# Biases added by TensorE from one table of three bfloat16 parts, in a graph layer with a routed feed-forward net

## The chip, the cores and the metric

The kernel runs on one core of a Trainium2 chip. The metric is the device time of one execution in microseconds (us). The engines have short names in the profile: PE (TensorE, matmuls), PEld (its weight loads), DVE (VectorE), ACT (ScalarE), POOL (GpSimd), SP (SyncE, here only a queue for transfers).

## What is computed

A graph with 3125 nodes of 256 features and 100,000 edges, sorted by destination, goes through one layer. Cut to what matters:

```python
xn = layernorm(x)
# graph part: a maximum over the edges of each node
e   = relu((xn[dst] - xn[src]) @ theta_w.T + theta_b + xn[src] @ phi_w.T + phi_b)
gnn = segment_max(e, dst)                 # 0 where a node has no edge
# mixer: attention without softmax, k and v normalised per head
mix = ((q @ (k.T @ v)) / N) @ w_out.T + b_out
x = x + gnn + mix
# feed-forward: 8 experts, the best 2 of each node, weighted
xt = layernorm(x)
logits = xt @ Wr + br
h = gelu((xt * ln_g[e] + ln_b[e]) @ W1[e] + b1[e])
y = h @ W2[e] + b2[e]
x = x + sum over the two experts of weight * y
```

Everything is float32. The biases that TensorE adds are `theta_b + phi_b`, `b_out`, `br` and the eight rows of `b2`.

## The kernel before

**Edges.** The part of an edge that depends on its source, b = xn @ (phi - theta).T, is a table in device memory (`b_d`). Each edge is a gathered row of it. A partition holds a run of consecutive edges, so a running maximum along the run, cut where the destination changes, gives each node's maximum. The edges stand in 727 columns of 128 edges, in five groups (`STEPS`), from the high nodes to the low ones. POOL gathers one column with one indirect transfer (L123) into one of five buffers of eight columns. DVE folds it into the running maximum (`fold`, L403), and SP's queue stores the full buffer to `s_d`. A buffer is free for the next gathers when its store has landed. A last set of 55 columns, of the 16 nodes with the most edges, is not gathered at all: `first_nodes` counts them by one-hot matmuls (L1119 to L1123) and `first_maxima` takes their maxima with mask matmuls in bfloat16 (L1173) and reductions on DVE (L1144).

**Nodes.** The 25 tiles of 128 nodes are taken group by group as their edges are done (`GROUPS`: tiles 18 to 24, 11 to 17, 4 to 10, 1 to 3, and 0). `mixer` (L1203 to L1231) sums k.T @ v over all tiles at the start and `mixer_product` folds it with the weights into `am_w`. `without_edges` (L439) then makes for a tile, in one PSUM bank of 512 columns, the part of the graph result that doesn't depend on edges (left half) and x plus the mixer's result (right half). It starts with the bias matmul of L444, which has one row, a weight of ones; then come four passes with `am_w` (L446) and two with the identity and x (L447). ACT copies both halves out (L450, L451). For groups 0 and 1 this runs right after the mixer's product, before the tokens; for the others after group 1's dispatch (`rest_without_edges`), before most of group 1's expert units. `token_tile` (L468) gathers the tile's last rows (`r1`), adds what was carried over between partitions (L492), normalises, and makes the router's logits, with a bias matmul of one row at L543.

**Experts.** Groups 0 to 2 are scattered by expert to device memory (L130) and come back as lots of 256 rows; group 3 is picked on chip by one-hot matmuls (L787), 128 rows for each expert; tile 0 goes densely through all eight experts. So there are 24 units of 256 rows (0 to 23), 8 of 128 (24 to 31) and 8 dense ones. A unit (`Units.run`, L685) has 8 steps; each makes 128 hidden features with matmuls into `hp` (L693) that ACT passes through gelu into `ring` (L695), and one step of the second layer of the unit before into `yp` (L717). When a `yp` is full, `done` (L875) adds the row of `b2` with a float32 matmul of 8 rows at L878: a column of the identity, spread over n columns, picks the expert. ACT copies the result to `ys` (L879), and ACT's queue stores it. The dense tile adds its biases in another way, with the shares as weights (L949).

**Order.** The order on PE, DVE, ACT and SP is the order in which the program text runs. A small planner writes it: the main loop issues a gather, moves its clock on by one tick (`TICK` is 1.25 us) and lets every task that is due issue its next instructions (`tick`, L1266). A task yields how many ticks it wants to wait. `on_pe(us)` books time on PE, and the stream of expert units (`Stream.go`, L843) yields `room()` after each step, the ticks until PE's booked time less two. So what is booked for `without_edges` (3.1 us at L448) moves the expert units in the order. Nothing is booked for the matmul of L878. POOL's gathers and scatters keep the order of issue (`behind`, L103), and so do all transfers made by `move` (L113).

**Loads.** `loads` (L1032) brings the small tensors through ACT's queue; after 20 ticks two DVE instructions (L1046, L1047) put together the bias row of `without_edges`.

Of the kernel before, what the change touches and what calls it, by code (L numbers as in the profile page):

```python
# [8 lines left out]
F32 = mybir.dt.float32  # L9
BF16 = mybir.dt.bfloat16  # L10
# [9 lines left out]
P = 128  # L20
# [4 lines left out]
D = 256  # L25
# [5 lines left out]
E = 8  # L31
# [32 lines left out]
SEATS = 3  # L64
TICK = 1.25
ROWS = 256

KEYS = 391
KR = EP // KEYS
# [2 lines left out]


@with_exitstack
def gps_layer(ctx: ExitStack, tc: tile.TileContext, x, src, dst, thetaT, phiT, gbias, wq, wkvT,
              woT, bout, wr, br, small, w12, b2, out):
    nc = tc.nc
    keep = ctx.enter_context(tc.tile_pool(name="keep", bufs=1))
    dram = ctx.enter_context(tc.tile_pool(name="dram", bufs=1, space=DRAM))
# [6 lines left out]
    def on_pe(us):  # L86
        clock["pe"] = max(clock["pe"], clock["now"]) + us / TICK
# [127 lines left out]
    to_node = keep.tile([P, G, NT], F32, name="to_node")  # L215
    through = keep.tile([P, G, P], BF16, name="through")
    am_w = keep.tile([P, 2, 2 * D], F32, name="am_w")
    bias = keep.tile([1, 2 * D], F32, name="bias")
    wr_sb = keep.tile([P, 2, E], F32, name="wr_sb")
    br_sb = keep.tile([1, E], F32, name="br_sb")  # L220
    b2_sb = keep.tile([E, D], F32, name="b2_sb")
    sm = keep.tile([P, SM, E], F32, name="sm")
    table = keep.tile([P, 1], F32, name="table")
# [210 lines left out]
    def last_rows(work, i, table):  # L434
        r1 = work.tile([P, D], F32, name="r1", bufs=4)
        gather(r1, table, end_i[:, i:i + 1])
        return r1

    def without_edges(ps, i):  # L439

        if ps is mm:
            yield from seat()
        am = ps.tile([P, 2 * D], F32, name="mm")
        nc.tensor.matmul(am, ones[0:1, :], bias, start=True, stop=False)  # L444
        for c in range(2):
            nc.tensor.matmul(am, xnT(i, c), am_w[:, c, :], start=False, stop=False)  # L446
        nc.tensor.matmul(am[:, D:2 * D], ident, x_sb[:, i, :], start=False, stop=True)  # L447
        on_pe(3.1)  # L448
        yield 3
        nc.scalar.copy(xn2(i), am[:, 0:D])  # L450
        nc.scalar.copy(x_sb[:, i, :], am[:, D:2 * D])  # L451
        if ps is mm:
            leave()
# [14 lines left out]
    def token_tile(work, ps, i, r1, slices, carried, top, top_i, newton=False, then=None,  # L468
                   also=None, at_once=None):


        xi = x_sb[:, i, :]

        def after(ticks):
            return min(ticks, at_once) if at_once else ticks

        picks = []
        for g in slices:
            picks.append(work.tile([P, P], F32, name="oh", bufs=G))
            nc.vector.tensor_scalar(picks[-1], apart, to_node[:, g, i:i + 1], None, op0=OP.is_equal)  # L480
        yield after(3)
        if also is not None:
            while "rows" not in also or "firsts" not in clock:
                yield 0.5
            nc.vector.tensor_max(r1, r1, also["rows"])
            nc.vector.tensor_max(r1[0:FIRST, :], r1[0:FIRST, :], of_first)
        yield from seat()
        r2 = ps.tile([P, D + 1], F32, name="mm")
        for k, g in enumerate(slices):
            while g not in carried:  # L490
                yield 1
            nc.tensor.matmul(r2, picks[k], carried[g], start=(k == 0), stop=(k == len(slices) - 1))  # L492
        on_pe(0.65 * len(slices))
        yield after(3)
        none = work.tile([P, 1], F32, name="none")
        nc.vector.tensor_scalar(none, r2[:, D:D + 1], -1.0, -NEG, op0=OP.add, op1=OP.mult)  # L496
        nc.vector.scalar_tensor_tensor(r1, r2[:, 0:D], none, r1, op0=OP.add, op1=OP.max)
        leave()
        nc.vector.tensor_add(r1, r1, xn2(i))
        yield 1  # L500
        nc.vector.scalar_tensor_tensor(xi, r1, 0.0, xi, op0=OP.max, op1=OP.add)  # L501
        yield 1
        mean, var = moments(work, xi, 1)

        rs = work.tile([P, 2], F32, name="rs1")
        nc.vector.tensor_scalar(rs[:, 0:1], var, EPS, None, op0=OP.add)
        nc.vector.reciprocal(rs[:, 1:2], rs[:, 0:1])
        nc.vector.tensor_scalar(rs[:, 1:2], rs[:, 1:2], var, EPS, op0=OP.mult, op1=OP.add)
        if newton:
            y = work.tile([P, 2], F32, name="root")  # L510
            for wait in roots(work, rs, y):
                if at_once != 1:
                    yield wait
            rs = y
        else:
            nc.scalar.activation(rs, rs, AF.Sqrt)
            yield after(4)
            nc.vector.reciprocal(rs, rs)
        off = work.tile([P, 1], F32, name="off")
        nc.vector.scalar_tensor_tensor(off, mean, -1.0, rs[:, 0:1], op0=OP.mult, op1=OP.mult)  # L520
        xt = work.tile([P, D], F32, name="xt")
        nc.scalar.activation(xt, xi, AF.Identity, bias=off, scale=rs[:, 0:1])
        if then:
            both = work.tile([P, 1], F32, name="both")
            nc.vector.tensor_mul(both, rs[:, 0:1], rs[:, 1:2])
            normalize(xn2(i), xi, mean, both)
            then()
        else:
            nc.scalar.activation(xn2(i), xt, AF.Copy, scale=rs[:, 1:2])
        yield after(3)  # L530
        yield from seat()
        tr = ps.tile([P, 2, P], F32, name="mm")
        for c in range(2):
            nc.tensor.transpose(tr[:, c, :], xt[:, c * P:(c + 1) * P], ident)
        on_pe(0.6)
        yield after(3)
        xtT = work.tile([P, 2, P], F32, name="xtT", bufs=1)
        nc.scalar.copy(xtT, tr)
        leave()
        yield after(2)  # L540
        yield from seat()
        lg = ps.tile([P, E], F32, name="mm")
        nc.tensor.matmul(lg, ones[0:1, :], br_sb, start=True, stop=False)  # L543
        for c in range(2):
            nc.tensor.matmul(lg, xtT[:, c, :], wr_sb[:, c, :], start=False, stop=(c == 1))
        on_pe(0.5)
        yield after(4)
        nc.vector.max(top, lg)
        nc.vector.max_index(top_i, top, lg)
        leave()  # L550
# [179 lines left out]
    class Stream:  # L730
# [112 lines left out]
        def go(self):  # L843
# [5 lines left out]
            while True:  # L849
# [21 lines left out]
                g, e = self.lots[u]  # L871
# [3 lines left out]
                def done(r, yp, u=u, ys=ys):  # L875
                    g, e = self.lots[u]
                    n = self.half(u)
                    nc.tensor.matmul(yp[0:n, :], ident[0:E, e:e + 1].to_broadcast([E, n]), b2_sb, start=False, stop=True)  # L878
                    nc.scalar.copy(ys[0:n, r, :], yp[0:n, :])  # L879
                    if r == PARTS[g] - 1:  # L880
                        at = (g * ROUND if g < G - 2 else 0) + e * CAPS[g]
                        rows = ys_d[g][at:at + CAPS[g]].rearrange("(p s) d -> p s d", p=n)
                        move(nc.scalar, rows, ys[0:n, 0:PARTS[g], :])
                        if u + 1 == len(self.lots) or self.lots[u + 1][0] != g:
                            self.through.add(g)
# [29 lines left out]
    def dense_tile(act, ps, mm, i, shared, w, next_w, order=range(E), ready=None, homes=None):  # L915
# [28 lines left out]
            nc.vector.tensor_copy(bt, bt_p)  # L944
            held["bt"] = bt

        def add_bias():
            bb = mm.tile([P, D], F32, name="mm")
            nc.tensor.matmul(bb, held["bt"], b2_sb, start=True, stop=True)  # L949
            nc.vector.tensor_add(x_sb[:, i, :], x_sb[:, i, :], bb)  # L950

        units = Units(ps, act, True)
        for k, e in enumerate(order):
            def done(r, yp, k=k, e=e):
                if k == 0:
                    nc.vector.tensor_scalar(o, yp, full[:, e:e + 1], None, op0=OP.mult)
                else:
                    nc.vector.scalar_tensor_tensor(o, yp, full[:, e:e + 1], o, op0=OP.mult, op1=OP.add)

            between = {1: lambda k=k: scaled(k + 1)}  # L960
            if k == 1:
                between.update({3: second_bias, 5: add_bias})
            if k > 1:
                between[1] = lambda k=k: (next_w(k - 2), scaled(k + 1))
            while k == 1 and not shared:
                yield 1
            for _ in units.run(e, w[e][0], held["xe", e], w[e][1], done, between, 1, P):
                yield 1
# [60 lines left out]
    ok = ea.tile([P, 1], F32, name="ok")  # L1029
    cuts(dstI, 0, STEPS[0])  # L1030

    def loads():  # L1032

        am_b = ea.tile([1, 3 * D], F32, name="am_b")
        move(nc.scalar, am_b[:, 0:D], bout)
        move(nc.scalar, am_b[:, D:3 * D], gbias)
        move(nc.scalar, wr_sb, wr.rearrange("(c p) e -> p c e", p=P))
        move(nc.scalar, br_sb, br)
        move(nc.scalar, b2_sb, b2)
        move(nc.scalar, sm, small)  # L1040
        low = ea.tile([1, D], F32, name="low")
# [1 line left out]
        zero = ea.tile([P, 1, D], F32, name="zero")  # L1043
        nc.vector.memset(zero, 0.0)
        yield 20
        nc.vector.tensor_add(bias[:, 0:D], am_b[:, D:2 * D], am_b[:, 2 * D:3 * D])  # L1046
        nc.vector.tensor_copy(bias[:, D:2 * D], am_b[:, 0:D])  # L1047
        yield 10
        move(nc.scalar, s_d[0:1, :], low)
        kept = s_d[1 + P * COL[G - 1]:1 + P * COL[G], :].rearrange("(p t) d -> p t d", t=STEPS[G - 1])  # L1050
# [211 lines left out]
    def start(task, at=None):  # L1262
        clock["tasks"] += 1
        tasks.append([clock["now"] if at is None else at, clock["tasks"], task])
# [474 lines left out]
```

## Time and profile before

| what | us |
|---|---|
| median of the runs | 1193.51 |
| lowest and highest of 3 runs | 1192.21, 1200.18 |
| the profiled execution's own time | 1687.79 |
| its span, first to last instruction | 1685.9 |
| bias matmuls L878 (yp), 112 passes, busy | 42.3 |
| bias matmuls L444 (trf, then mm), 28 and 22 passes, busy | 20.4 and 13.4 |
| bias matmuls L543 (logits), 50 passes, busy | 11.5 |

A float32 matmul shows as two passes, so 112 passes are 56 matmuls. The profile comes from one execution, and that one was much longer than the runs; durations of single instructions and the order can be read from it, while the waits between them belong to that execution. The granted clock of PE, on average, was 0.772 of the full one. Busy times of PE overlap, since matmuls are pipelined; what a matmul costs is better read from start to start.

### The profile page before, as it was taken

The page shows a single profiled execution, that of the slowest core. Times are in us where ns is not written, and L with a number is a line of the kernel's source. Part 1 is how long each engine was busy: PE and PEld are TensorE (multiplying, and loading weights), DVE is VectorE, ACT ScalarE, POOL GpSimd, SP SyncE. Part 2 cuts the span into 40 slices and gives each one's busy share as a digit, 9 for nine tenths or more (in the row PEclk, how much of TensorE's full clock was granted, in tenths as well). Part 3 has the DMA queues.
Part 4 walks back from the last instruction along what each step waited for, and adds up shares of the span by engine and source line. Part 5 has one row for each costly group of instructions (what it writes and reads, how often), then busy time and mean ns, then how long its engine had stood idle before and what let it go on. Part 6 is the DMA issues. An engine that isn't in the chain of part 4 may idle for free.

```text
span 1685.9 us, 14751 instructions
## 1 busy us (share of the span) xinstructions
PE 1036.5 (61%) x4385; PEld 736.8 (44%) x4385; DVE 786.6 (47%) x2571; ACT 327.0 (19%) x787; POOL 846.9 (50%) x879
## 2 busy tenths in 40 slices
PE   3515766455671285963986783864066838869877
PEld 2402433232230164752554662643054626657666
DVE  3647956372445134730454561768264415433332
ACT  1301222110220021310111220211021204223222
POOL 6274554666537735464254627445743464632251
PEclk7757989776765576995987986975587858879898
DMA  7344555485536435773263875544445755539462
GB/s 230 126 123 146 182 193 186 146 300 207 175 147 224 157 125 176 245 261 90 79 215 112 287 265 159 182 138 174 141 162 196 249 163 182 185 131 331 149 243 94
DMA packets 102595, 306.72 MB, mean 182 GB/s; under 512 B 20518, under 2 KB 44190, under 8 KB 91625
## 3 DMA queue, kind: packets, MB, share of 16 engines
q0 software_dynamic: 42400, 115.28, 22.2%
q1 hardware_dynamic: 29164, 109.58, 17.0%
q10 hardware_dynamic: 30940, 80.82, 14.2%
q8 instruction: 37, 0.61, 0.1%
q14 instruction: 54, 0.43, 0.1%
HBM read 184.84 MB, written 120.75 MB: 181 GB/s over the span
## 4 chain that ended last, share of the span: by engine, by line
PE 44%; another core or an unknown queue 24%; DVE 13%; issue 10%; POOL 4%; ACT 3%; DMA 1%; ACTq 0%; POOLq 0%; DVEq 0%; SPq 0%
PE hp L693 14%; PE yp L717 11%; DVE g L403 4%; POOL g L123 3%; PE v L1207 2%; PE yp L878 2%; PE bp L278 2%; DVE xn_hi L1144 1%; PE trf L446 1%; PE mm L446 1%; PE k L1207 1%; ACT ring L695 1%; PE mm L1173 1%; PE mm L492 1%
## 5 line engine op out<-in xcount | busy, mean ns | idle before, releaser
L123 POOL DMA_INDIRECT g<-b_d,srcI x727 | 703.7, 968 | 556.8 <-issue 213.5
L403 DVE SCALAR_TENSOR_TENSOR g<-g,cut 128x256 f32<-128x256 f32 x722 | 348.3, 482 | 67.4 <-DMA g<-b_d,srcI 34.0
L695 ACT ACTIVATE ring<-hp,sm 128x256 f32<-128x256 f32 (+1 forms) x320 | 136.7, 431 | 636.8 <-PE hp L693 280.8
L1144 DVE CUSTOM_DVE_ANT_0 xn_hi<-xn_hi,mm 128x512 bf16<-128x512 f32 (+1 forms) x224 | 140.4, 627 | 237.7 <-PE mm L1173 118.8
L693 PE MATMUL hp<-xe,big 128*128 128x256 f32 (+1 forms) x768 | 191.8, 377 | 66.7 <-issue 48.0
L693 PE MATMUL hp<-xe,w 128*128 128x256 f32 (+1 forms) x448 | 121.3, 403 | 174.5 <-issue 99.7
L717 PE MATMUL yp<-big,ring 128*128 128x256 f32 x624 | 186.7, 420 | 3.5 <-issue 3.4
L693 PEld LDWEIGHTS hp<-xe,big 128*128 128x128 f32 x768 | 138.0, 208 | 95.8 <-issue 57.9
L693 PEld LDWEIGHTS hp<-xe,w 128*128 128x128 f32 x448 | 85.8, 220 | 199.7 <-issue 109.6
L717 PEld LDWEIGHTS yp<-big,ring 128*128 128x128 f32 x624 | 125.8, 212 | 27.5 <-issue 10.4
L717 PE MATMUL yp<-w,ring 128*128 128x256 f32 x368 | 108.6, 412 | 0.0
L1173 PE MATMUL mm<-ident_h,absent 128*128 128x128 bf16 x400 | 45.7, 240 | 77.1 <-DVE xn_hi L1144 18.6
L717 PEld LDWEIGHTS yp<-w,ring 128*128 128x128 f32 x368 | 73.1, 210 | 12.5 <-issue 3.0
L1173 PEld LDWEIGHTS <-absent 128*128 128x128 bf16 x400 | 33.2, 108 | 88.4 <-issue 20.7
L123 POOL DMA_INDIRECT g<-ys_d,from_i x42 | 40.7, 968 | 55.8 <-DMA out<-g 27.7
L123 POOL DMA_INDIRECT r<-s_d,end_i x25 | 23.7, 948 | 82.7 <-DVE x_sb L501 46.3
L1207 PE MATMUL v<-wkv,xn_hi 128*128 128x512 f32 x56 | 35.0, 756 | 49.0 <-ACT big L1212 46.0
L1216 DVE TENSOR_REDUCE var<-big 128x16 f32<-128x1024 f32 x25 | 30.4, 1216 | 65.7 <-ACT big L1213 38.9
L130 POOL DMA_INDIRECT xs_d<-xn_hi,slot_i x28 | 30.5, 1088 | 54.6 <-issue 30.1
L496 DVE TENSOR_SCALAR none<-mm 128x1 f32<-128x1 f32 x25 | 3.9, 156 | 109.8 <-PE mm L492 59.3
L416 DVE TENSOR_TENSOR_SCAN ct<-through,ct,mm 128x128 f32<-128x128 bf16 x8 | 3.4, 467 | 106.4 <-remote 80.4
L808 ACT ACTIVATE xe<-trf,sm 128x256 f32<-128x256 f32 (+1 forms) x64 | 30.8, 535 | 91.3 <-PE trf L797 57.0
(318 smaller groups left out, 1397.7 us busy)
## 6 DMA issues: line engine op xcount, KB each, us to landing
s_d<-g SPq DMA_DIRECT2D x75, 1024.0 KB
big<-in_w ACTq DMA_DIRECT2D x48, 512.0 KB
w<-in_w ACTq DMA_DIRECT2D x32, 512.0 KB
s_d<-g SPq DMA_DIRECT2D x13, 896.0 KB
g<-b_d,srcI POOLq DMA_INDIRECT x727
big<-in_w ACTq DMA_DIRECT2D x4, 2048.0 KB
xs_d<-zero ACTq DMA_DIRECT2D x24, 256.0 KB
xn_hi<-xs_d ACTq DMA_DIRECT2D x12, 512.0 KB
```

The source lines that it names most:

```text
L123: got = nc.gpsimd.indirect_dma_start(out=to, out_offset=None, in_=table, in_offset=row_index(index))
L278: nc.tensor.matmul(bp, xnT(i, c), wb[:, c, :], start=(c == 0), stop=(c == 1))
L403: nc.vector.scalar_tensor_tensor(g[:, j, :], last, cut[:, t:t + 1], g[:, j, :], op0=OP.add, op1=OP.max)
L446: nc.tensor.matmul(am, xnT(i, c), am_w[:, c, :], start=False, stop=False)
L693: nc.tensor.matmul(hp[:, 0:n], w1t[:, c, f, :], xe[:, c, 0:n], start=(c == 0), stop=(c == 1))
L695: nc.scalar.activation(hT[f][:, 0:n], hp[:, 0:n], AF.Gelu, bias=sm[:, 4 + f, e:e + 1])
L717: nc.tensor.matmul(yp[r][0:part, :], hT[q][:, r * part:(r + 1) * part], w2t[:, q, :], start=(q == 0), stop=(q == FC - 1 and self.whole))
L808: nc.scalar.activation(xe[:, c, 0:n], self.held["tr", u][:, c, 0:n], AF.Identity, bias=sm[:, 2 + c, e:e + 1], scale=sm[:, c, e:e + 1])
L878: nc.tensor.matmul(yp[0:n, :], ident[0:E, e:e + 1].to_broadcast([E, n]), b2_sb, start=False, stop=True)
L1144: nc.vector.tensor_tensor_reduce(unread[:, 0:n * P], bT[:, h, 0:n * P], mask_p[:, 0:n * P], 1.0, NEG, op0=OP.add, op1=OP.max, accum_out=mo ...
L1173: nc.tensor.matmul(mask_p[:, i * P:(i + 1) * P], absent[:, at:at + 1].to_broadcast([P, P]), ident_h, start=True, stop=True)
L1207: nc.tensor.matmul(to, xnT(i, c), wkv[:, c, k * INNER:(k + 1) * INNER], start=(c == 0), stop=(c == 1))
```

## The change

All these biases go into one input of 74 rows and 520 columns, `biases`. It holds the same ten rows three times, at rows 0, 32 and 64: eight rows of `b2`, a row with `theta_b`, `b_out` and `br`, and a row with `phi_b`; the rows between are zero. One load brings it. On the chip `split_biases` turns the three copies into three bfloat16 parts whose sum is the float32 number: the rounded value, the rounded rest, and the rounded rest of that (`thirds`). A second table, `which_bias`, has nine columns of zeros and ones: column e picks row e of each copy, and column 8 both other rows. A bias is then added by one bfloat16 matmul: a column of `which_bias`, spread over n columns, times the wanted columns of `thirds`. This takes the place of L444, L543 and L878; L949 and `b2_sb` stay. The booking for `without_edges` becomes 2.3.

```diff
+APART_3 = 32
+ROWS_3 = 2 * APART_3 + E + 2
...
-    bias = keep.tile([1, 2 * D], F32, name="bias")
+    thirds = keep.tile([ROWS_3, 2 * D + E], BF16, name="thirds")
+    which_bias = keep.tile([ROWS_3, E + 1], BF16, name="which_bias")
...
-    br_sb = keep.tile([1, E], F32, name="br_sb")
...
+    def add_bias(to, k, n, cols, start, stop):
+
+        nc.tensor.matmul(to, which_bias[:, k:k + 1].to_broadcast([ROWS_3, n]), thirds[:, cols], start=start, stop=stop)
+
     def without_edges(ps, i):
...
-        nc.tensor.matmul(am, ones[0:1, :], bias, start=True, stop=False)
+        add_bias(am, E, P, slice(0, 2 * D), True, False)
...
-        on_pe(3.1)
+        on_pe(2.3)
...
-        nc.tensor.matmul(lg, ones[0:1, :], br_sb, start=True, stop=False)
+        add_bias(lg, E, P, slice(2 * D, 2 * D + E), True, False)
...
-                    nc.tensor.matmul(yp[0:n, :], ident[0:E, e:e + 1].to_broadcast([E, n]), b2_sb, start=False, stop=True)
+                    add_bias(yp[0:n, :], e, n, slice(0, D), False, True)
...
+    def split_biases(of_biases):
+
+        nc.vector.tensor_copy(thirds, of_biases)
+        nc.vector.memset(which_bias, 0.0)
+        for k in range(3):
+            at = k * APART_3
+            of = slice(at, at + E + 2)
+            nc.vector.tensor_copy(which_bias[of, 0:E], ident_h[of, at:at + E])
+            nc.vector.tensor_add(which_bias[of, E:E + 1], ident_h[of, at + E:at + E + 1], ident_h[of, at + E + 1:at + E + 2])
+            yield 1
+        for first in (1, 2):
+            for k in range(first, 3):
+                of = slice(k * APART_3, k * APART_3 + E + 2)
+                nc.vector.tensor_sub(of_biases[of], of_biases[of], thirds[of])
+                nc.vector.tensor_copy(thirds[of], of_biases[of])
+                yield 1
+
     def loads():
 
-        am_b = ea.tile([1, 3 * D], F32, name="am_b")
-        move(nc.scalar, am_b[:, 0:D], bout)
-        move(nc.scalar, am_b[:, D:3 * D], gbias)
+        of_biases = ea.tile([ROWS_3, 2 * D + E], F32, name="of_biases")
+        move(nc.scalar, of_biases, biases)
         move(nc.scalar, wr_sb, wr.rearrange("(c p) e -> p c e", p=P))
-        move(nc.scalar, br_sb, br)
...
-        nc.vector.tensor_add(bias[:, 0:D], am_b[:, D:2 * D], am_b[:, 2 * D:3 * D])
-        nc.vector.tensor_copy(bias[:, D:2 * D], am_b[:, 0:D])
+        start(split_biases(of_biases))
```

The other edits rename a function of the dense tile and build the new input.

## The prediction

> **What bounds the kernel now.** I read the page first, then the stretches of time, then single instructions. The profiled execution took 1687.8 us (span 1685.9 us and 1.9 us around it). The median of the runs is 1193.5 us. The profiled one is therefore 494 us longer than what I have to predict, and this decides how its numbers may be used.
>
> ```profile
> PE 1036.5 (61%) x4385; PEld 736.8 (44%) x4385; DVE 786.6 (47%) x2571; ACT 327.0 (19%) x787; POOL 846.9 (50%) x879
> ...
> PEclk7757989776765576995987986975587858879898
> ...
> PE 44%; another core or an unknown queue 24%; DVE 13%; issue 10%; POOL 4%; ACT 3%; DMA 1%; ACTq 0%; POOLq 0%; DVEq 0%; SPq 0%
> ```
>
> The chain that ended last spends 24% on an unknown queue and 10% on "issue": 0.34 x 1686 = 573 us with no cause in the program. An example is a stretch near 760 to 787 us in which PE, DVE and ACT stand still and only POOL goes on. A run of 1193 us cannot hold all of these holes. So I take durations and pitches (start to start) from the trace, and not its waits.
>
> POOL first. Its gathers start 1.25 us apart (second column: duration; the bracket: idle before).
>
> ```profile
> 1548.64 0.95 POOL L123 DMA_INDIRECT g<-ys_d,from_i  x1 [0.30 <-issue]
> 1549.89 0.95 POOL L123 DMA_INDIRECT g<-ys_d,from_i  x1 [0.30 <-issue]
> ```
>
> The edge gathers average 968 ns, so 1.27 us with the gap. Up to the last edge gather POOL issues 727 edges, 24 row gathers and 42 scatters: 793 x 1.27 = 1007 us. The first edge gather starts at 72.9 us. So POOL alone brings us to 1080 us of 1191.6 (1193.5 - 1.9), with some 112 us left for what follows: tile 0, the last expert units, the dense tile.
>
> PE second. At full clock a float32 matmul of 256 columns takes 0.43 us (two passes). The planner (`on_pe`, TICK 1.25) books PE nearly full from unit 16 (the first of group 2, tick 634, PE booked to 633.3) to unit 31 (tick 803, booked to 806.6): 173 booked ticks against 169 elapsed. It books nothing for the bias matmuls of L878. POOL and PE are close to co-critical, and the end (dense units, 7.0 us each) is PE work.
>
> **The change, part by part.** First the bias of the second layer (L878, 56 times). The row around one of them, in a unit of group 3:
>
> ```profile
> 1520.99 0.60 PE L717 MATMUL yp<-big,ring 128*128 128x256 f32 x2
> 1521.52 0.69 PE L878 MATMUL yp<-b_sb,ident 8*128 8x256 f32 x2
> 1522.14 0.71 PE L693 MATMUL hp<-xe,w 128*128 128x128 f32 x4
> 1522.69 0.60 PE L717 MATMUL yp<-big,ring 128*128 128x256 f32 x2
> 1523.12 0.61 PE L693 MATMUL hp<-xe,w 128*128 128x128 f32 x4
> 1523.57 0.60 PE L717 MATMUL yp<-big,ring 128*128 128x256 f32 x2
> ```
>
> From yp to yp it is 1.70 us with the bias between and 0.88 without: the bias costs 0.82 us, not 0.43, because PE drains around it. The new one is one bfloat16 pass of 256 columns over 74 rows. No such row exists; the nearest is the bfloat16 mask matmul on 128 rows among float32 ones:
>
> ```profile
> 930.37 1.03 PE L717 MATMUL yp<-big,ring 128*128 128x256 f32 x4
> 931.24 0.39 PE L1173 MATMUL mm<-ident_h,absent 128*128 128x128 bf16 x4
> 931.46 1.08 PE L693 MATMUL hp<-xe,big 128*128 128x256 f32 x4
> 932.38 1.03 PE L717 MATMUL yp<-big,ring 128*128 128x256 f32 x4
> ```
>
> Four of 128 columns hold PE for 0.22 us, and the hp behind them takes 0.92 instead of 0.86. So 256 columns: 0.11 + 0.06 = 0.17 us. Saved: 0.65 us each, 36 us of PE in all.
>
> Here a rule can be weighed. The Trainium skill, "TensorEngine Tiling (Array Packing)", Key Properties, says that a change of tiling mode, not just of the tile, drains TensorE, and its modes have 32, 64 or 128 rows. The 0.33 us that the weight load stands idle on both sides of L878 (8 rows) fits this; 74 rows fit only the 128-row mode, so by the rule the drain goes and 0.17 us holds. If the drain stays, as the row of L878 itself would have it, the new one costs 0.17 + 0.39 = 0.56 and saves 0.26. I take 0.17, as the mask row shows no gap, and keep 0.56 for the range.
>
> The bias of `without_edges` (L444, 25 times): from 809.96 (four transposes, 0.43) to 813.36 lie 3.40 us, of which L446 needs 4 x 0.427 = 1.71. So it costs 1.26 us, the new one 0.21 + 0.06 = 0.27; 0.99 saved, 25 us in all. All 25 lie before tick 430, while PE has gaps behind them until tick 621 (group 1's units end near 550): worth nothing by itself. The router's (L543, 25 times): about 0.4 to 0.12, 7 us in all, of which only tiles 1, 2, 3 and 0 come late, 1.2 us.
>
> What is on the path: a unit of group 2 is 32 x 0.43 + 0.44 (transposes L797) + 2 x 0.82 = 15.84 us; booked are 32 x 0.43 + 1.2 = 14.96. A unit of group 3 takes 9.19 us (1522.14 to 1531.33); booked are 16 x 0.43 + 1.5 = 8.38. So PE falls behind its plan by 8 x 0.88 + 8 x 0.81 = 13.5 us before the dense tile, and in the plan there is no slack to catch up. Tile 0's transposes, the picks of the last rows and the dense units stand in PE's order behind these units and inherit the lag. With the change the units take 14.54 and 8.54: the lag is at most 8 x 0.16 = 1.3 us. On the path: 12.2 us saved (with the drain kept, 24 x 0.26 = 6.2).
>
> The planner's number for `without_edges` falls from 3.1 to 2.3, so the FFN stream moves up: unit 8 stands at tick 423 instead of 433, group 1's last at 525 instead of 534. The hp, yp, ring copies and the ACT queue's weight and row loads of units 8 to 15 move with it, past 11 bias-and-copy pairs and mask steps; order on POOL and SP is the same, and from group 2 on that on PE and ACT too. PE really needs 2.6 us per tile there after the change, so 2.3 is honest, and I cost the move at nothing; the cover is the gap of ticks 550 to 621 (70 us).
>
> What is added: 13 DVE instructions near tick 21 to 27 in place of two (0.41 + 0.27 us). By nearest rows: the copy of 74 x 520 (0.42 per 256 columns) 0.8; memset 0.1; six tiny ones at 0.15, 0.9; three subtractions at 0.7 (TENSOR_TENSOR of 512 columns) and three copies at 0.6, 3.9. With overlap of 0.08 each, 4.7 - 0.7 = 4.0 us net. The bounds are 2.5 and 5. Behind them on DVE wait the folds (L403), whose stores free the row buffers that POOL gathers into. DVE is full just then:
>
> ```profile
> 150.00:200.00 50.00, 38.06 (x139) 19.13 (x137) 48.35 (x169) 9.81 (x22) 24.00 (x25) 0.96 0.55 189
> ```
>
> That is 48.35 of 50 us on DVE (third pair of numbers), and POOL issued 25 where 39 would fit: 8.3 us went by in one wait for L388, 7.4 in one for L1119. Cover is the five buffers of 8 gathers (50 us less the lag of 6 ticks and the store). In the profile a late DVE had used it up; in a run without holes it is about even. I take half: 2 us. On ACT's queue one load of 154 KB replaces three small ones, some 20 ticks before use: nothing.
>
> A rule that speaks against the change: "TensorE: Matmul & The Clock Gate", section on HAM oscillation, says that an idle gap over about 3.4 us puts the clock to half. The trace: after 4.11 us idle at 1579.01 the pairs run at half pitch until about 1587; at full clock that stretch would save some 4 us. If the freed PE time gathered into such gaps, each would give back 4 us. I expect gaps of under 2 us between units, because units are paced to 2 ticks, and count none.
>
> Sum: -12.2 + 2 = -10 us, 1183.5 us.
>
> **Rivals.** *POOL hides it.* If POOL's issue and tile 0's row gather, not PE's lag, set when the dense tile starts, only the router's bias of tile 0 (0.3 us) and up to 4 us of DVE count: 1191 to 1197. For: 793 x 1.27 alone is 1007 us. Against: the last gathers leave 112 us, and PE needs about 56 for dense units after 20 for tile 0 and its neighbours.
> *The start decides, slower.* The split sits in DVE's full stretch; POOL loses 4 to 5 us there and never makes it up. It decides from the point at which PE's lag on the path is under 4 us: 1198; up to 1210 if the mixer's steps queued behind it (L1216, L1225) delay group 0's tiles too. Against: half of the cover should remain.
> *PE bounds more.* If tokens and masks wait for PE in groups 1 and 2 as well, their folds reach POOL late and the 16 units before also count: 12.2 + 16 x 0.65 = 22.6; with other gains 18 to 27, 1167 to 1175. For: PE holds 44% of the chain. Against: the gap before tick 621.
>
> **Numbers.** The main case has 0.55 (its own range 1177 to 1190), POOL hiding 0.18, the slower start 0.13, PE bounding more 0.14. About 1% (11.9 us) is what a measurement can tell here; the three runs spread over 0.7%. Faster by over 1% (below 1181.6): 0.22 of the main case and all 0.14 of the last, 0.36. Slower by over 1%: 0.06 of the start's 0.13. Within: 0.58. The range 1166 to 1201 leaves out about 0.1.
>
> **What would show it.** A yp-to-yp distance with a bias of about 1.05 us instead of 1.70, with no idle weight load around it; units of group 3 at 8.5 us instead of 9.19; the bias groups falling from 42, 34 and 11.5 us busy to under 15 each. If the distance is 1.4 the drain stayed. If units are shorter and the time is not, POOL hid it; if POOL's waits for DVE before 210 us grow, the start took it. I am wrong above all if the lag of PE never reaches the dense tile in an undisturbed run.

## The result and the profile after

| | kernel before | changed kernel |
|---|---|---|
| median of 7 runs each, us | 1193.51 | 1183.14 |
| lowest and highest, us | 1191.14, 1200.18 | 1182.48, 1188.65 |
| ratio, with its 95% interval | | 0.9915 [0.9889, 0.9942] |

The change makes the kernel 0.85% faster, 10.4 us by the medians. The forecast was 1183.5, with 0.58 for a change of less than 1%. The size was right. The way to it was right only in part, which is what the experiments are about.

The first profile of the kernel before held some 500 us of stretches in which nothing moved (1687.8 us). Profiled a second time, the same kernel took 1187.56 us (span 1185.8), near its runs; this second profile stands for it from here on. It is on the fast side: the median of the kernel before was 1190 to 1193 us in every later comparison. First its busy times, granted clock by fortieths, and the shares of the chain that ended last:

```profile
PE 933.5 (79%) x4385; PEld 680.9 (57%) x4385; DVE 786.4 (66%) x2571; ACT 328.5 (28%) x787; POOL 855.2 (72%) x879
...
PEclk9768999958875589899989999875599999999899
...
PE 41%; DVE 20%; DMA 19%; POOL 9%; issue 8%; ACT 2%; ACTq 0%; DVEq 0%; POOLq 0%; SPq 0%
```

The same of the changed kernel (1182.51 us, span 1180.7):

```profile
PE 869.3 (74%) x4279; PEld 668.5 (57%) x4279; DVE 791.1 (67%) x2583; ACT 325.9 (28%) x787; POOL 857.1 (73%) x879
...
PEclk9768999968785589899999999955589989999899
...
PE 29%; DMA 24%; DVE 20%; POOL 15%; issue 9%; ACT 1%; ACTq 0%; POOLq 0%; DVEq 0%; SPq 0%
```

The unknown queue, 24% of the chain in the first profile, is gone in both. PE is busy for 64 us less, its share of the chain falls from 41% to 29%, and DMA and POOL take it over: 64 us less busy time of PE gave 10 us. Now one bias matmul in a unit of group 3 of the changed kernel, with its neighbours:

```profile
1040.21 0.60 PE L723 MATMUL yp<-big,ring 128*128 128x256 f32 x2
1040.64 0.28 PE L443 MATMUL yp<-thirds,which_bias 74*128 74x256 bf16 x1
1040.76 0.61 PE L699 MATMUL hp<-xe,w 128*128 128x128 f32 x4
1041.20 0.60 PE L723 MATMUL yp<-big,ring 128*128 128x256 f32 x2
```

From yp to yp it is 0.99 us, where it was 1.70: the bias costs 0.11 us. A unit of group 3 with no wait takes 8.48 us (1040.76 to 1049.24) instead of 9.19. The bias groups are busy for 15.8 us (yp), 10.4 (the graph part) and 4.5 (router) instead of 40.4, 31.7 and 11.3.

### The profile page after: what moved, and what is told of

Its sections match the earlier page's. It is cut to its first block, busy times and chain, and to the rows that moved or that the text cites. A ratio compares the mean times of both kernels' runs of the same rounds, so it can differ in the third digit from the quotient of the medians.

```text
span 1180.7 us, 14516 instructions
## 1 busy us (share of the span) xinstructions
PE 869.3 (74%) x4279; PEld 668.5 (57%) x4279; DVE 791.1 (67%) x2583; ACT 325.9 (28%) x787; POOL 857.1 (73%) x879
## 4 chain that ended last, share of the span: by engine, by line
PE 29%; DMA 24%; DVE 20%; POOL 15%; issue 9%; ACT 1%; ACTq 0%; POOLq 0%; DVEq 0%; SPq 0%
DMA g<-b_d,srcI 17%; POOL g L125 13%; PE hp L699 7%; PE yp L723 7%; DVE g L405 6%; PE v L1227 3%; DMA r<-s_d,end_i 3%; PE k L1227 2%; POOL xs_d L132 2%; PE bp L280 2%; DVE xn_hi L1164 2%; DMA big<-in_w 2%; PE dots_p L1250 1%; PE mm L498 1%; DMA xs_d<-zero 1%
## 5 line engine op out<-in xcount | busy, mean ns | idle before, releaser
L125 POOL DMA_INDIRECT g<-b_d,srcI x727 | 715.3, 984 | 223.1 <-issue 190.3
L699 PE MATMUL hp<-xe,big 128*128 128x256 f32 (+1 forms) x768 | 176.9, 355 | 4.4 <-DMA big<-in_w 2.9
L723 PE MATMUL yp<-big,ring 128*128 128x256 f32 x624 | 164.8, 381 | 0.0
L699 PEld LDWEIGHTS hp<-xe,big 128*128 128x128 f32 x768 | 131.9, 199 | 21.1 <-ACT ring L701 2.6
L723 PEld LDWEIGHTS yp<-big,ring 128*128 128x128 f32 x624 | 113.1, 192 | 14.3
L699 PE MATMUL hp<-xe,w 128*128 128x256 f32 (+1 forms) x448 | 105.4, 364 | 6.3 <-DMA w<-in_w 3.1
L803 PE MATMUL trf<-ident,xn_hi 128*128 128x128 f32 x96 | 15.6, 288 | 54.5 <-DMA xn_hi<-xs_d 54.5
L498 PE MATMUL mm<-cr,oh 128*128 128x257 f32 x118 | 38.8, 466 | 21.8 <-DVE top_i L555 8.2
L803 PEld LDWEIGHTS trf<-ident,xn_hi 128*128 128x128 f32 x96 | 12.5, 149 | 57.0 <-DMA xn_hi<-xs_d 54.9
L498 PEld LDWEIGHTS mm<-cr,oh 128*128 128x128 f32 x118 | 25.9, 233 | 28.8 <-issue 12.3
```

The lines of the kernel that those rows point to most:

```text
L125: got = nc.gpsimd.indirect_dma_start(out=to, out_offset=None, in_=table, in_offset=row_index(index))
L699: nc.tensor.matmul(hp[:, 0:n], w1t[:, c, f, :], xe[:, c, 0:n], start=(c == 0), stop=(c == 1))
L723: nc.tensor.matmul(yp[r][0:part, :], hT[q][:, r * part:(r + 1) * part], w2t[:, q, :], start=(q == 0), stop=(q == FC - 1 and self.whole))
```

## Where the saved time went, by the two traces

**The same up to tile 0.** POOL's gathers run level in both, within some 2 us: its last edge gather starts at 1069.63 us before and 1071.63 after, its gather of tile 0's rows at 1074.43 and 1074.61. The first pick of group 3 (`trf`) starts only 2.1 us earlier (1007.23, 1005.14), since PE waits for group 3's one-hot masks in front of it (3.3 us instead of 1.9, near 967) and runs at a granted clock of 0.50 behind that wait, so that the eight matmuls there take 3.8 us instead of 2.0. The eight units after it save 8 x 0.71 = 5.7 us, and yet tile 0's transposes start at 1096.34 before and 1096.03 after. Each of these units needs 2 MB of weights, which come in four transfers of 512 KB. The waits of PE for them, in the kernel before:

```profile
1065.13 0.46 PE L693 MATMUL hp<-xe,big 128*128 128x128 f32 x2 [1.78 <-DMA big<-in_w]
...
1075.71 0.46 PE L693 MATMUL hp<-xe,w 128*128 128x128 f32 x2 [0.73 <-DMA w<-in_w]
```

and in the changed kernel, with the matmuls behind the first of them:

```profile
1051.86 0.46 PE L699 MATMUL hp<-xe,big 128*128 128x128 f32 x2 [2.24 <-DMA big<-in_w]
1052.16 0.60 PE L723 MATMUL yp<-w,ring 128*128 128x256 f32 x2
1052.59 0.66 PE L699 MATMUL hp<-xe,big 128*128 128x128 f32 x4
1053.04 1.06 PE L723 MATMUL yp<-w,ring 128*128 128x256 f32 x2
1053.90 1.06 PE L699 MATMUL hp<-xe,big 128*128 128x128 f32 x4
...
1075.12 0.46 PE L699 MATMUL hp<-xe,w 128*128 128x128 f32 x2 [3.09 <-DMA w<-in_w]
```

With a third wait on each side (0.32 before, 0.65 after) the sums are 2.8 and 6.0 us. Faster units only reach the weights' arrival earlier: the lead of 3.2 us at the start of one unit (1043.92 before, 1040.76 after) is 0.6 us behind the last of these waits (1075.71, 1075.12). And the clock falls: 1.2 us after the wait of 2.24 us the pairs take 0.85 us instead of 0.43, up to 1056.4 (granted clock 0.50), which costs 1.7 us more. The stretch from 1050 to 1060 us (its columns: length, then busy time of PE, PEld, DVE, ACT and POOL, the granted clock, the DMA share and GB/s), of the kernel before:

```profile
1050.00:1060.00 10.00, 9.68 (x67) 8.50 (x66) 4.69 (x12) 3.90 (x11) 7.56 (x9) 1.00 1.04 404
```

and of the changed one:

```profile
1050.00:1060.00 10.00, 8.14 (x47) 7.59 (x48) 5.49 (x15) 2.09 (x6) 7.64 (x8) 0.83 1.03 417
```

All DMA engines are busy in both (share 1.04 and 1.03), and they move little more in the changed one. The chain of waits says the same. First the line on most of these transfers in the page of the changed kernel (number, size, median us from issue to landing):

```profile
big<-in_w ACTq DMA_DIRECT2D x48, 512.0 KB, 8.7
```

Of its chain from 1050 to 1077 us, start and length:

```profile
1052.36 10.38 DMA big<-in_w
...
1063.38 11.60 DMA w<-in_w
```

Each piece is one transfer of 512 KB, the one that PE waited for, from its issue to its landing; three others lie between one and the next. The two landings (1062.74 and 1074.98) are 12.2 us apart and the pair before them 11.0, so 2 MB took 11 to 12 us where PE's unit needs 8.5. In the kernel before (pieces of 8.95, 10.57 and 9.95 us) the landings are 11.2 and 10.6 us apart, where PE's unit needs 9.2. So transfers bound group 3's stage in both kernels, and the faster units only wait longer.

**The gain comes after that.** From tile 0's transposes to the last matmul it is 83.05 us before and 78.20 after. Three places make it. First, PE has stood still for over 4 us before these transposes (tile 0's chain on DVE) and runs at half clock behind them (granted clock 0.50 in both), where the pairs take 0.85 us instead of 0.43. The kernel before:

```profile
1096.34 0.69 PE L534 MATMUL mm<-ident,xt 128*128 128x128 f32 x2 [4.11 <-ACT xt L522]
1096.96 1.22 PE L878 MATMUL yp<-b_sb,ident 8*128 8x256 f32 x2
1098.11 1.22 PE L693 MATMUL hp<-xe,big 128*128 128x128 f32 x4
...
1100.11 0.59 PE L543 MATMUL mm<-br_sb,ones 1*128 1x8 f32 x2
1100.63 1.02 PE L545 MATMUL mm<-wr_sb,xtT 128*128 128x8 f32 x4
1101.51 0.67 PE L920 MATMUL mm<-ident,xn_lo 128*128 128x128 f32 x2
```

The changed one:

```profile
1096.03 0.69 PE L540 MATMUL mm<-ident,xt 128*128 128x128 f32 x2 [4.39 <-ACT xt L528]
1096.51 0.42 PE L443 MATMUL yp<-thirds,which_bias 74*128 74x256 bf16 x1
1096.72 1.06 PE L699 MATMUL hp<-xe,big 128*128 128x128 f32 x4
...
1098.43 0.21 PE L443 MATMUL mm<-thirds,which_bias 74*128 74x8 bf16 x1
1098.50 1.02 PE L551 MATMUL mm<-wr_sb,xtT 128*128 128x8 f32 x4
1099.38 0.67 PE L926 MATMUL mm<-ident,xn_lo 128*128 128x128 f32 x2
```

The bias of a unit takes 1.15 us here before (1096.96 to 1098.11) and 0.21 after, the router's 0.52 and 0.07; from L534 to the transposes of the dense tile 5.17 us become 3.35. Second, the stretch with the last two biases of group 3, from the dense tile's transposes to its own first matmuls (13.25 us, then 12.41), saves 0.8 us: the two biases save 1.3, and half clock lasts 0.5 us longer there. Third, the first of the dense units whose weights come late. Before:

```profile
1155.79 0.60 PE L717 MATMUL yp<-g,ring 128*128 128x256 f32 x2
1160.02 1.19 PE L693 MATMUL hp<-xe,w 128*128 128x128 f32 x4 [3.63 <-issue]
1161.00 1.06 PE L717 MATMUL yp<-big,ring 128*128 128x256 f32 x2
```

After:

```profile
1155.86 0.70 PE L699 MATMUL hp<-xe,w 128*128 128x128 f32 x4 [2.21 <-issue]
1156.40 0.60 PE L723 MATMUL yp<-big,ring 128*128 128x256 f32 x2
```

The wait is 1.4 us shorter, and in the kernel before, at half clock (granted clock 0.50), the matmuls up to 1163.48 take 3.46 us for what takes 1.85 at full clock. This third part is partly chance: over the ten profiles in which these weights come in one piece and no load is left out, the wait was 2.2 to 9.0 us.

Together that is 1.8 + 0.8 + 1.4 + 1.6 = 5.6 us. The changed kernel gives 0.7 us back in two waits for ACT's `ring` that are longer than before (0.2 near 1113, 0.5 near 1163), which leaves the 4.9 found. So this pair of profiles differs by 5 us; the medians differ by 7.5 to 10. The rest is the fast execution that the second profile of the kernel before caught, and this pair can't say where it lies.

## The experiments

The time before is the median of 43 to 51 runs on the same chip. The ratio compares runs of the same rounds, with its 95% interval; it can lie up to 0.25% under the quotient of the medians.

| kernel | median, us | before, us | ratio |
|---|---|---|---|
| before_again (one run) | 1187.56 | 1190.19 | |
| late_only | 1188.61 | 1190.19 | 0.9975 [0.9959, 0.9991] |
| early_only | 1186.90 | 1190.19 | 0.9967 [0.9952, 0.9982] |
| split_only | 1192.74 | 1190.19 | 1.0019 [0.9999, 1.0038] |
| after_again | 1183.54 | 1191.01 | 0.9934 [0.9915, 0.9953] |
| tail_only | 1192.01 | 1191.01 | 1.0003 [0.9982, 1.0023] |
| upto_28 | 1188.30 | 1191.01 | 0.9965 [0.9945, 0.9985] |
| halves | 1178.21 | 1191.01 | 0.9883 [0.9847, 0.9919] |
| before_no_w | 1189.64 | 1193.02 | 0.9970 [0.9952, 0.9987] |
| after_no_w | 1174.89 | 1193.02 | 0.9832 [0.9800, 0.9865] |
| rows128 | 1190.53 | 1193.02 | 0.9973 [0.9955, 0.9992] |
| booked31 | 1184.38 | 1193.02 | 0.9904 [0.9873, 0.9935] |

**before_again**: the kernel before, unchanged.

> The kernel before once more, for a profile without the holes of the first one. If the lag of PE is what the change removes, POOL runs through at 1.27 us a gather up to its last edge gather near 1072 us, while PE comes to the transposes of the last group's carry (L411) at about 1095 us or later, some 10 us behind the changed kernel's 1085.5, with no long wait in the units of groups 2 and 3. If POOL is what the change shortened, its last edge gather comes some 10 us later than in the changed kernel and waits for DVE or stores stand before it.

It gave the profile used above. The sign of the lag did not come: the transposes of L411 start at 1086.04 us, 0.6 us behind the changed kernel's 1085.45 and not 10.

**Parts of the change alone.** All three load both sets of tables and make the split. `late_only` takes the new table only for units 16 to 31, `early_only` for everything but these, `split_only` for nothing. The core of `late_only` (in `early_only` the condition is `u < 16`; `split_only` keeps the old line):

```diff
-                    nc.tensor.matmul(yp[0:n, :], ident[0:E, e:e + 1].to_broadcast([E, n]), b2_sb, start=False, stop=True)
+                    if u >= 16:
+                        add_bias(yp[0:n, :], e, n, slice(0, D), False, True)
+                    else:
+                        nc.tensor.matmul(yp[0:n, :], ident[0:E, e:e + 1].to_broadcast([E, n]), b2_sb, start=False, stop=True)
```

> Only the second-layer biases of units 16 to 31 (groups 2 and 3) come from the bfloat16 table; all other biases and the booking are as before. Theory (PE's lag from unit 16 on): nearly the whole gain of the change, 8 to 12 us faster than before. Rival (PE held up tokens and masks earlier as well): about half of the gain. Rival (the gain comes from the earlier order of the units or from the tiles without edges): no gain.

> All biases from the table and the new booking, but units 16 to 31 keep the float32 matmul of 8 rows. Theory: 0 to 2 us faster than before (the router's biases of the late tiles), or up to 2 us slower by the split on DVE. Rivals: at least half of the gain of 10 us.

> The table is loaded and split on DVE as in the change, but no matmul uses it; the old biases are loaded and added as before. It has the cost of the split alone, without the saving of what it replaces. If DVE's cover is half gone: 2 us slower than before; fully gone: 4 to 5 us; if the row buffers cover it: 0 within 1 us.

The split alone costs 2.3 us (ratio 1.0019; its interval runs from nothing to 4.5 us). Measured against `split_only`, the late units bring 4 to 5 us and the early part 6. The forecast had 12, and no more than 1.2 us of late routers. Against the kernel before, `late_only` is 3 us ahead by its ratio, where 8 to 12 were expected, and `early_only` 3.9, where at most 2 were. The parts do add up (2.3 - 5.2 - 6.2 = -9 us by the ratios), but it is not where I put it.

**The changed kernel again, its last part alone, and all but its last part.** `tail_only` uses the table for the units 29, 30, 31 and tile 0's router only, `upto_28` for everything else. The core of `tail_only` (in `upto_28` the conditions are `u < 29` and `i > 0`):

```diff
-                    add_bias(yp[0:n, :], e, n, slice(0, D), False, True)
+                    if u >= 29:
+                        add_bias(yp[0:n, :], e, n, slice(0, D), False, True)
+                    else:
+                        nc.tensor.matmul(yp[0:n, :], ident[0:E, e:e + 1].to_broadcast([E, n]), b2_sb, start=False, stop=True)
...
-        add_bias(lg, E, P, slice(2 * D, 2 * D + E), True, False)
+        if i == 0:
+            add_bias(lg, E, P, slice(2 * D, 2 * D + E), True, False)
+        else:
+            nc.tensor.matmul(lg, ones[0:1, :], br_sb, start=True, stop=False)
```

> The changed kernel once more, beside the partial ones. Inherited lag (the forecast: units 16 to 31 save 12 us, the split costs 2) and the tail theory (those units' savings are taken back by waits for tokens and weights; what counts is the work after tile 0's transposes, plus something early) both expect the 8 to 10 us of the first comparison again. If it is 5, as between the two undisturbed profiles, the rest was chance between calls.

> bfloat16 biases only for the units 29, 30, 31 and for tile 0's router logits; all others float32, booking 3.1; both sets of tables are loaded and the split is made. Inherited lag: 3 x 0.65 + 0.3 = 2.3 us saved, about 2 paid for the split: 0 against the kernel before. Tail theory: 4 to 5 us saved, 2 paid: -2 to -3.

> The complement of tail_only: everything from the new table with booking 2.3, except that units 29, 30, 31 and tile 0's router logits keep float32. Inherited lag: all but 2.3 of the gain stays, -7 to -8 us against the kernel before. Tail theory: as the kernel with float32 biases in units 16 to 31 (measured -4): -3 to -5.

The changed kernel is 7.9 us ahead again (ratio 0.9934). `upto_28` is 4.2 us ahead, as much as `early_only` (3.9): turning units 16 to 28 to the new table brings nothing that can be measured (two such ratios can differ by some 3 us by chance), and the three last units and tile 0's router bring the 3.7 us (by the ratios; 4.8 by the medians of the same chip) between `upto_28` and the whole change. On its own, `tail_only` does not differ from the kernel before, as the inherited lag expected and not the tail theory; it gains only 1.9 us against `split_only`, which is within chance. Its profile shows L534 to the dense tile's transposes in 3.34 us, as after, but a wait of 3.9 us for the dense weights behind it. So the tail brings its share when the rest of the change is there; why it does not alone is not shown.

**Without the weight loads.** If weights take the savings of group 3 back, the savings must come out when these loads are left out, in both kernels (units 25 to 31 then compute with the weights that the slots hold):

```diff
-            for e, k in self.loads.get(q, ()):
-                self.held["w", k] = load_w(self.wts[k], e, nc.scalar, parts)
+            for e, k, at in self.loads.get(q, ()):
+                if at >= 25:
+                    w = self.wts[k]
+                    self.held["w", k] = first_of(w[:, 0:HALF]), second_of(w[:, HALF:2 * HALF])
+                else:
+                    self.held["w", k] = load_w(self.wts[k], e, nc.scalar, parts)
```

> The kernel before, with the weight loads of the units 25 to 31 left out (7 x 2 MB; these units compute with what the slots hold, so their results are not the layer's). In its profile PE waits 2.8 us in all for these weights. Weights bound the stage: 3 to 4 us faster than the kernel before. Not bound by them: 0 to 1 (the wait goes to POOL's last edge gathers and tile 0's rows instead).

> The changed kernel, with the same loads left out. In its profile PE waits 6.0 us in all for these weights. If the savings of units 24 to 31 (8 x 0.7 us) are only taken back by these waits, they come out now: 14 to 16 us faster than the kernel before, that is 5 to 6 faster than the changed kernel, and 11 to 12 faster than the kernel before without these loads. If something else (POOL's last gathers, tile 0's chain) takes the savings back too, it is only as much faster than the other as with the loads, 8 to 10.

The kernel before gains 3.4 us by it, the changed kernel 9.5 (1174.89 against 1184.38 for `booked31` on the same chip, which stands for it), more than the 5 to 6 expected: the waits of 6.0 us and the half clock of 1.7 make 7.7 of it. Between the two it is now 14.8 us by the medians, where it is 7.5 to 10 with the loads. Tile 0's transposes, in `before_no_w`:

```profile
1092.76 0.69 PE L534 MATMUL mm<-ident,xt 128*128 128x128 f32 x2 [4.11 <-ACT xt L522]
```

in `after_no_w`:

```profile
1086.62 0.44 PE L540 MATMUL mm<-ident,xt 128*128 128x128 f32 x2 [4.25 <-ACT xt L528]
```

They start 6.1 us earlier, not 0.3, though POOL's gather of tile 0's rows is level again (1070.68, 1070.98). So PE's lag does reach the dense tile, as the forecast said, unless the weights stand in between. This is shown: the two kernels differ in nothing but the change. (The profile of `before_no_w` is its fastest run, 1183.83 us; against its median the lead would be larger.) If the early part and the split make 3.9 us of the 14.8, as in `early_only`, the late units make about 11, near the 12.2 of the forecast; that is an estimate. These runs do not separate the rate of the transfers from the moment of their issue; the DMA share of 1.03 speaks for the rate.

**The drain.** `rows128` keeps float32 and only gives the bias matmul 128 rows instead of 8, padded with zeros:

```diff
-    b2_sb = keep.tile([E, D], F32, name="b2_sb")
+    b2_all = keep.tile([P, D], F32, name="b2_sb")
+    nc.vector.memset(b2_all, 0.0)
+    b2_sb = b2_all[0:E, :]
...
-                    nc.tensor.matmul(yp[0:n, :], ident[0:E, e:e + 1].to_broadcast([E, n]), b2_sb, start=False, stop=True)
+                    nc.tensor.matmul(yp[0:n, :], ident[:, e:e + 1].to_broadcast([P, n]), b2_all, start=False, stop=True)
```

> The kernel before, with the second layer's biases still float32 at L878, but the table padded with zeros to 128 rows, and the picking column from the whole identity. If the 8 rows make TensorE drain (0.33 us on both sides of the matmul), the bias costs 0.43 to 0.45 us here instead of 0.82: yp to yp 1.31 instead of 1.70, and about half of the path's gain from the units, 2 to 3 us, without any split. If the price is that of two float32 passes and something else, it stays at 1.70 and the time at that of before.

Its bias in a unit of group 3:

```profile
1043.11 0.60 PE L719 MATMUL yp<-big,ring 128*128 128x256 f32 x2
1043.54 0.59 PE L880 MATMUL yp<-b_sb,ident 128*128 128x256 f32 x2
1043.97 0.61 PE L695 MATMUL hp<-xe,w 128*128 128x128 f32 x4
1044.42 0.60 PE L719 MATMUL yp<-big,ring 128*128 128x256 f32 x2
```

From yp to yp it is 1.31 us: with sixteen times the rows the bias costs 0.43 us instead of 0.82. So half of the old price was the number of rows, not the float32. Four changed lines without any new input bring 2.5 us.

**The order.** `booked31` is the changed kernel with `on_pe(3.1)`.

> The changed kernel with the booking for the graph part put back to 3.1, so that the expert units 8 to 15 stand where they stood before in the order. Forecast: the move is worth nothing, so the same as the changed kernel, -8 to -10 against before. If the move is what the kernel with float32 biases in units 16 to 31 gained by (it was 6 us ahead of the one with only the split): 3 to 6 us slower than the changed kernel, -3 to -6 against before.

1184.38 us, 8.6 ahead of the kernel before by the medians: the move of units 8 to 15 in the order is worth nothing that can be measured, as forecast.

**A faster kernel.** `halves` is the changed kernel with the weights of the last three dense units loaded in two halves; a slot's first-layer half is free one unit before its second half:

```diff
-            if k > 1:
-                between[1] = lambda k=k: (next_w(k - 2), scaled(k + 1))
+            if k > 0:
+                between[1] = lambda k=k: (next_w(k), scaled(k + 1))
...
-        if k < 3:
-            e = DENSE[k + 5]
-            dense_w[e] = load_w(at_hand["w"][dense_slot[k]], e, nc.scalar)
+        for j, half in ((k - 2, 1), (k - 1, 0)):
+            if 0 <= j < 3:
+                e = DENSE[j + 5]
+                of = slice(half * HALF, (half + 1) * HALF)
+                dense_half(e, half, at_hand["w"][dense_slot[j]][:, of], nc.scalar)
```

> The changed kernel, but the weights of the last three dense units are loaded in halves, the first-layer half one unit earlier (as soon as its slot's first half is free). The profile of the changed kernel shows PE waiting 2.2 us for these weights near 1156 us (3.6 us in the kernel before, and half clock after it). If that wait is what bounds the dense stage: about 2 us faster than the changed kernel, and PE's wait there under 0.5. If the transfers are bound by the DMA rate there, no change.

Its profile where the wait was:

```profile
1149.26 0.60 PE L723 MATMUL yp<-g,ring 128*128 128x256 f32 x2
1149.69 0.61 PE L699 MATMUL hp<-xe,w 128*128 128x128 f32 x4
1150.13 0.60 PE L723 MATMUL yp<-big,ring 128*128 128x256 f32 x2
```

No wait is left there, and from L540 to the last matmul it takes 75.6 us instead of 78.2. The median is 1178.21 us, 5.3 under the changed kernel and 12.8 under the kernel before: the fastest kernel of the study that leaves nothing out. It is more than the 2 us of one profile's wait; the wait was longer in most other profiles (2.6 in `after_again`, 3.6 in `booked31`, where the same stretch takes 80.0 and 79.3 us). The two profiled executions differ by 6.1 us, but 3.5 of these lie in front of L540 (1092.56 instead of 1096.03), where the order on PE, DVE and ACT is the same in both kernels: that part is chance, and of the 5.3 us by the medians the profiles show 2.6 to 4.4 in their place.

## Why the prediction was right, and where not

**Right in size.** The bias of L878 was costed at 0.82 us, 0.17 with the change; it is 0.11. The 74-row bfloat16 matmul lies wholly inside the stream, without the 0.06 us that I took for its way in. The rule on tiling modes (the Trainium skill, "TensorEngine Tiling (Array Packing)", Key Properties: a change of mode drains TensorE) was the right choice against the row of L878. `rows128` shows the price of the 8 rows alone, 0.43 against 0.82 us; that it is a drain, as the rule says, no run shows by itself. The units went from 9.19 to 8.48 us (forecast 8.54). The bias groups should each have fallen to under 15 us busy; yp's is 15.8. The split was put at 4.0 us net, of which 2 on the path; it measures 2.3. Its instructions, fourteen and not the thirteen counted, are busy for 4.9 us, most of it here (its subtractions and casts; minimum, median and maximum in ns):

```profile
L1051 DVE TENSOR_TENSOR of_biases<-of_biases,thirds x3: 694/741/756, 89.7 to 97.2; 10x520 f32<-10x520 f32 x3
L1052 DVE CAST thirds<-of_biases x3: 421/434/434, 90.5 to 98.0; 10x520 bf16<-10x520 f32 x3
```

POOL's 146th indirect transfer starts 1.2 us later than before (207.7 against 206.5), so the cover hid most of the split there; later in this pair POOL is level again. The order move was put at nothing, and `booked31` agrees.

**The step that failed** is "On the path: 12.2 us saved", with "in the plan there is no slack to catch up". With the loads, the late units bring 4 to 5 us. The lag was real, and without the weight loads the two kernels are 14.8 us apart. But transfers stood in front of PE: in the kernel before, the weights landed 10.6 to 11.2 us apart, with PE's unit at 9.19, and so the lag reached tile 0 as no more than 0.3 us in the undisturbed pair, which is where the prediction said that it would be wrong above all. I had worked out PE and POOL for group 3's stage and not the third resource. The sum that was missing: 2 MB in 8.5 us are 247 GB/s, POOL's gathers (128 KB in 1.27 us) 103, and the stores of the folded rows as much again: 453 GB/s (434 at the old 9.19 us), where the stretch shows 404 to 417 at a full DMA share. So the rival that I should have written was "weights hide it".

**"count none"** was the other miss, on the clock. The Trainium skill, "TensorE: Matmul & The Clock Gate", HAM oscillation, puts the danger at idle gaps over about 3.4 us, and I took gaps under 2 us as safe. In the changed kernel a wait of 2.24 us is followed by 3.3 us at half clock, which costs 1.7 us, while one of 3.09 us (1075.12) is followed by none. In the kernel before, 3.63 us in the dense stage costs 1.6 us more than the wait itself. So the length of the wait alone does not decide in these traces. The clock worked both ways here: it took back part of the gain in group 3, and in tile 0's stretch it had raised the price of a unit's old bias from 0.62 us (1062.23 to 1062.85) to 1.15.

**What made up for it.** The early part (L444, the router, units 0 to 15), put at nothing, brings some 6 us against `split_only`. It is not the order (`booked31`). Whether it is L444 or units 0 to 15 was not tried and stays open. On the wait there is a hint. POOL's gather of tile 0's rows in `split_only`:

```profile
1082.13 0.94 POOL L125 DMA_INDIRECT r<-s_d,end_i  x1 [7.70 <-DMA w<-in_w]
```

and in `early_only`:

```profile
1074.33 0.94 POOL L125 DMA_INDIRECT r<-s_d,end_i  x1 [4.32 <-DMA w<-in_w]
```

It starts at 1077.2 to 1082.1 us in the three profiles that have the split and float32 biases early, at 1071.6 to 1075.4 in the six that have both new, and at 1074.2 and 1074.4 in the two without the split. So the early part and the split seem to reach the end through POOL's side; with one profile for most kernels this is not shown. That the sum came out near -10 is luck: the late part was put 7 us too high and the early part 6 too low.

**The rivals.** "POOL hides it" had a point up to 1074 us, where POOL's gathers are level in both kernels; but PE, not POOL, releases tile 0's chain after that. "The start decides, slower" expected 4 to 5 us, and `split_only` shows 2.3. "PE bounds more" was right that the units before also count. Its sum is too small by its own terms, since a unit of 256 rows adds two biases: 12.2 + 32 x 0.65 = 33 us; measured are 10, and 14.8 without the weights.

## What to carry to other kernels

Before a saving on one engine is put on the path, add up the bytes of that stage as well: where transfers are as slow as the engine or slower, the saving becomes a wait for them, and half clock can follow on top. A small matmul among large ones is priced by start-to-start distance, not by its duration; if only its number of rows is odd, padding with zeros is the cheaper repair. When a buffer is filled by one large transfer, ask which half of it is free first: that brought 5 us by the medians here, half as much as the whole change.

## What the runs showed of the hardware

A bfloat16 matmul of 74 rows and 256 columns between float32 ones of 128 rows costs 0.11 us; a float32 one of 8 rows costs 0.82, of 128 rows 0.43. Half clock also comes without any wait. In the changed kernel, behind 24 passes of one column each (the last 16 are the first line; the granted clock from 1030 to 1032 us is 0.50):

```profile
1026.88 1.93 PE L1470 MATMUL mm<-ones,xn_hi 128*128 128x1 f32 x16
1028.67 0.79 PE L699 MATMUL hp<-xe,big 128*128 128x128 f32 x4
1029.26 1.06 PE L723 MATMUL yp<-w,ring 128*128 128x256 f32 x2
```

The kernel before in its second profile, at the same place (1.00 from 1032 to 1036):

```profile
1030.39 1.93 PE L1450 MATMUL mm<-ones,xn_hi 128*128 128x1 f32 x16
1032.18 0.69 PE L693 MATMUL hp<-xe,big 128*128 128x128 f32 x4
1032.70 0.60 PE L717 MATMUL yp<-w,ring 128*128 128x256 f32 x2
```

Ten of the thirteen profiles taken after the first one of the kernel before show the half clock there (with float32 biases too, as in `split_only`), three do not. It costs 1.7 us on PE and falls on the changed kernel in this pair; as it lies in front of the waits for weights, what of it reaches the end is not shown.
